# Normalised tiles of sequences one to three and seven k tiles turned by 32x32 blocks on VectorE, by way of DRAM, in a gated linear attention and MLP kernel

## The chip, the cores and the metric

The kernel runs on one core of one Trainium2 chip. A core has five engines with a queue each, and each takes its instructions in order: TensorE (PE in the profile: matrix products, and transposes as products with an identity; its weight loads are listed as PEld), VectorE (DVE), ScalarE (ACT), GpSimd (POOL) and SyncE (SP), which here issues every DMA. They wait for each other by semaphores. The metric is the device time of one execution in microseconds (us); the median of several executions is compared.

## The reference, cut to what matters

The input x has 4 sequences of 512 tokens with 512 features, in fp32. The layer is a chunked gated linear attention (4 heads of 128, chunks of 128 tokens), followed by a GEGLU MLP whose weights are 4-bit codes with scales. Both have a layer norm before them and a residual after.

```python
q = norm(x) @ Wq + bq;  k = norm(x) @ Wk + bk;  v = norm(x) @ Wv + bv     # 4 heads of 128
k = k / max(|k|, 1e-12)                        # per head
alpha = sigmoid(norm(x) @ Walpha + balpha);  beta = softplus(norm(x) @ Wbeta + bbeta)
# per chunk of 128 tokens, per head:
cla   = cumsum(log(alpha + 1e-6))
attn  = (qc @ kc.T) * beta.T * tril(exp(cla - cla.T))
y     = attn @ vc + (qc @ state.T) * exp(cla)
state = state * exp(cla_end) + vc.T @ (kc * beta * exp(cla_end - cla))
x1    = x + y
gate = norm(x1) @ Wg.T;  up = norm(x1) @ Wu.T            # 4096 wide
out  = x1 + (gelu_tanh(gate) * up) @ Wd.T
```

Two operands have to be turned for this, since TensorE contracts over partitions: a normalised tile (128 tokens on partitions by 512 features) is needed with the features on partitions, and so is a k tile (128 tokens by 4 heads of 128), for `qc @ kc.T`.

## The kernel before

The work is cut into 16 tiles of 128 tokens, (b, n) with b the sequence and n the chunk in it. The program is written in its final order by hand; nothing reorders it. The attention part runs steps p = 0 to 47: in sequence b, step 12b + j makes one product, `product_v(b, j)` for j = 0 to 3, `product_q(b, j - 4)` for j = 4 to 7, `product_k(b, j - 8)` for j = 8 to 11. After each product `behind(p)` places the rest of the work. The chunk with the running number c = 4b + n is worked off in steps 9 + 3c to 11 + 3c, by what p leaves when divided by three:

- p % 3 == 0: `chunk_lead` turns the chunk's k tile on TensorE (four transposes, L519, tile tpk) and ScalarE copies it to kT (L522); `chunk_decay` makes the decay matrix dm (ScalarE, GpSimd) and qc (GpSimd).
- p % 3 == 1: `turn` turns norm tiles on TensorE (L333: tp_f for the MLP's norm, tp_a for the first norm, four transposes each); ScalarE copies tp_a into hT (L348, two copies). `chunk_scores` (L586, tile sp) multiplies kT with q; VectorE multiplies the result with dm (L597). Loads of later tiles of x are issued here.
- p % 3 == 2: `chunk_sums` makes the state's update dp (L611) and the output yp (L640, L642); VectorE adds yp to the residual tile xr (L649), takes the second norm's statistics (L298 to L304), adds the state, and starts the first norm of a later tile (`first_norm`, L298 to L305). `settle` then normalises: hn_f and hn_a (L312). One slot of weight unpacking follows on VectorE (`unpack`, in the steps with p % 3 not 0, after p = 12), and then the next product's sums (L390 to L392 for v, L418 for k).

The first norm of a tile runs far ahead of its use: tile (1, n) in steps 2, 5, 8 and 8, tile (2, n) in steps 11, 14, 17 and 20, tile (3, n) in steps 23, 26, 29 and 32; their products begin in steps 12, 24 and 36.

SP's queue holds the DMAs in program order, and a DMA that waits holds all behind it. At most eight DMAs are under way: each one also waits for the eighth before it. SBUF tiles of 128x512 fp32 come from a list of 42 homes (`one_k`), taken from the front and given back at the end; PSUM has eight banks, taken in turn. From step 43 on the MLP is mixed in; it is a long run of products (L774, L818) with the weights unpacked beside them on VectorE.

Of the kernel before, what the change touches and what calls it, by code (L numbers as in the profile page):

```python
# [8 lines left out]
F32 = mybir.dt.float32  # L9
# [4 lines left out]
AF = mybir.ActivationFunctionType  # L14
ALU = mybir.AluOpType
# [6 lines left out]
P = 128  # L22
# [13 lines left out]
def f32(t):  # L36
    return t.bitcast(F32)
# [3 lines left out]
def tile_gated_linear_attention__then__nvfp4_geglu(  # L41
# [19 lines left out]
    nc = tc.nc  # L61
    B, T, D = x.shape
    H = D // P
    NCH = T // P
    NT = B * NCH
    KC = D // P
# [8 lines left out]
    dram = ctx.enter_context(tc.tile_pool(name="dram", bufs=1, space=DRAM))  # L75
# [199 lines left out]
    acc, hT, q_sb, k_sb, v_sb = {}, {}, {}, {}, {}  # L275
# [5 lines left out]
    def load(src, name):  # L281
        t = one_k.get(name)
        nc.sync.dma_start(f32(t), src)
        return t
# [7 lines left out]

    settled, turned = [], []

    def norm(src, key, use, parts=1, within=None):

        st = small.tile([P, 6], F32, tag="st", name=f"st_{key}")
        nc.vector.bn_stats(st, f32(src))  # L298
        if within:
            within()  # L300
        mv = small.tile([P, 2], F32, tag="mv", name=f"mv_{key}")
        nc.vector.bn_aggr(mv, st)
        rs = small.tile([P, 1], F32, tag="rs", name=f"rs_{key}")
        nc.vector.tensor_scalar(rs, mv[:, 1:2], 1e-5, None, ALU.add)  # L304
        nc.gpsimd.tensor_tensor(rs, rs, minus_half[:, :1], ALU.pow)  # L305

        def settle():

            hn = one_k.get(f"hn_{key}")
            w = D // parts  # L310
            for cols in (slice(i * w, (i + 1) * w) for i in range(parts)):
                nc.vector.tensor_scalar(  # L312
                    f32(hn)[:, cols].rearrange("p (c two j) -> p c two j", two=2, j=P),
                    f32(src)[:, cols].rearrange("p (c j two) -> p c two j", two=2, j=P),
                    mv[:, 0:1], rs, ALU.subtract, ALU.mult,
                )
            one_k.put(src)
            turned.append((hn, key, use))

        settled.append(settle)  # L320
# [6 lines left out]
    def turn(which, most=NT):  # L327
        for done in [t for t in turned if t[1][0] in which][:most]:
            turned.remove(done)
            hn, key, use = done  # L330
            tp = psum(f"tp_{key}")
            for k in range(KC):
                nc.tensor.transpose(tp[:, k * P : (k + 1) * P], f32(hn)[:, k * P : (k + 1) * P], ident)  # L333
            one_k.put(hn)
            use(tp)

    def first_norm(b, n, src, within=None):
        if n == 0:
            hT[b] = [two_k.get(f"hT{b}_{c}") for c in range(KC // 2)]

        soon = b == n == 0

        def use(tp):
            for c in range(KC // 2):
                to = f32(hT[b][c])[:, :, n * P : (n + 1) * P]
                new = tp[:, 2 * c * P : 2 * (c + 1) * P].rearrange("p (two t) -> p two t", two=2)
                for part in ((0, 1), (1, 2)) if soon else ((0, 2),):
                    nc.scalar.copy(to[:, slice(*part), :], new[:, slice(*part), :])  # L348

        norm(src, f"a{b}_{n}", use, 2 if soon else 1, within)  # L350

    def second_norm(b, n, src):
        def use(tp):
# [40 lines left out]
    def product_q(b, h):  # L394
# [10 lines left out]
            f32(q_sb[b][h // 2])[:, h % 2, :], pq, AF.Identity, bias=bq_sb[:, h : h + 1]  # L405
        )

    def product_k(b, n):

        pk = psum(f"pk_{b}_{n}")  # L410
        for k in range(KC):
            nc.tensor.matmul(  # L412
                pk, f32(hT[b][k // 2])[:, k % 2, n * P : (n + 1) * P], f32(wk[k // 2])[:, k % 2, :],
                start=(k == 0), stop=(k == KC - 1),
            )
        kt = one_k.get(f"k_{b}_{n}")
        k_sb[b, n] = kt
        nc.vector.tensor_tensor(f32(kt), pk, f32(bk_sb), ALU.add)  # L418
        return lambda: k_factors(b, n, kt)

    def k_factors(b, n, kt):
        sq = one_k.get(f"sq_{b}_{n}")
        sn = small.tile([P, H], F32, tag="ss", name=f"ss{b}_{n}")
        for h in range(H):
            hs = slice(h * P, (h + 1) * P)
            nc.scalar.activation(
                f32(sq)[:, hs], f32(kt)[:, hs], AF.Square, accum_out=sn[:, h : h + 1]
            )
# [74 lines left out]
    def gates_end(b):  # L503
        nc.vector.tensor_tensor(bdte[b], bdte[b], beta[b], ALU.mult)
# [8 lines left out]
    state, ch = {}, {}  # L513

    def chunk_lead(b, n):
        kT = one_k.get(f"kT_{b}_{n}")
        tp = psum(f"tpk_{b}_{n}")
        for h in range(H):
            nc.tensor.transpose(  # L519
                tp[:, h * P : (h + 1) * P], f32(k_sb[b, n])[:, h * P : (h + 1) * P], ident  # L520
            )
        nc.scalar.copy(f32(kT), tp)  # L522
        ch["kT"] = kT
# [38 lines left out]
    def chunk_values(b, n):  # L562

        brn, kwf = ss.pop((b, n))
        kt = k_sb[b, n]
        if n + 1 < NCH:
            kw = one_k.get(f"kw_{b}_{n}")
            nc.gpsimd.tensor_tensor(heads(f32(kw)), heads(f32(kt)), bc(kwf), ALU.mult)
# [129 lines left out]
    def behind(p):  # L698
        place[0] = p + 1
        b, j = divmod(p, 3 * NCH)  # L700
        chunk = chunk_of(p)
        first = b < B
        if not first:
            between_steps(p)
        left = chunk if p not in met else None
        if p % 3 == 0:
            if left:
                chunk_lead(*chunk)
            exps = gates_exp(b) if first and j == 3 else None
            if chunk and chunk[1] == 0:  # L710
                chunk_values(*chunk)
            if first and j == 6:
                exps = gates_sums(b)
            if left:
                chunk_decay(*chunk)
            if exps:
                exps()
        elif p % 3 == 1:
            turn("f")

            if p > 1:
# [12 lines left out]
        else:  # L734
            if first and j == 5:
                gates_ln(b)
            if chunk and not summed:
                sums, rest = chunk_sums(*chunk)
                sums()
                summed.append(rest)  # L740
            while summed:
                summed.pop()()
            for t in early.get(p, ()):
                first_norm(*t, xs.pop(t))
            if p + 1 < 3 * NCH * B:
                settle()
# [173 lines left out]
    with tc.manual_schedule():  # L920
# [3 lines left out]
        bv_sb, bk_sb = one_k.get("bv"), one_k.get("bk")  # L924
# [40 lines left out]
        blocks = mlp()  # L965
        p = 0
# [95 lines left out]
```

## Time and profile before

| what | value |
|---|---|
| median of 3 runs | 1308.09 us (1307.48 to 1310.34) |
| the profiled execution's own time | 1308.09 us |
| its span in the profile | 1306.1 us, 17024 instructions |
| TensorE busy | 1296.4 us, 99% |
| VectorE, ScalarE, GpSimd busy | 954.0 us (73%), 461.5 us (35%), 108.9 us (8%) |
| the three groups of transposes on TensorE (tp_a, tp_f, tpk) | 10.0, 9.7 and 9.6 us busy, 64 records each |
| ScalarE's copies of their results (hT, kT) | 10.3 us in 34, 9.3 us in 16 |
| DMA | 240.79 MB, mean 184 GB/s, 56.7% of 16 engines |

The profiled execution took the time of the median run, and its span leaves 2.0 us around it. A record's duration includes the time a product takes to run through the array, and that overlaps the next one: what a group of products takes from TensorE's row is the distance between starts, read in the order of time. Each fp32 transpose of 128x128 stands as two records in the groups, and as "x4" for four instructions in the order of time.

### The profile page before, as it was taken

Reading aid. Unit: us, or ns where it says so; the run is one execution under the profiler, and the core shown is the slowest. Engines: PE = TensorE matmul, PEld = TensorE weight load, DVE = VectorE, ACT = ScalarE, POOL = GpSimd, SP = SyncE. Lnnn points to the kernel's source line nnn. Section 1 sums busy time; section 2 is a strip of 40 time slices with the busy share of each in tenths; the row PEclk is TensorE's granted clock in tenths of the full one; section 3 lists DMA queues with packets and bytes.
Section 4 is the critical chain, followed back from the end, with each engine's and each line's share of the span. In section 5 each row is a group of like instructions: output and inputs, shape, how many; then the busy total and the mean of one; then the engine's idle time right before and its main releaser. Section 6 shows DMA issues by size and latency. Waiting matters only on the chain.

```text
span 1306.1 us, 17024 instructions
## 1 busy us (share of the span) xinstructions
PE 1296.4 (99%) x5808; PEld 1038.3 (79%) x5808; DVE 954.0 (73%) x1539; ACT 461.5 (35%) x908; POOL 108.9 (8%) x179
## 2 busy tenths in 40 slices
PE   9999999999999999999999999999999999999998
PEld 6677676778888888888888888888888888887886
DVE  3467665798777777777777777777777777777566
ACT  2443435753333333333333333333333333332332
POOL 1535263410000000000000000000000000000000
PEclk9999999999999999999999999999999999999999
DMA  5235446888555555555555555555555555555463
GB/s 194 82 108 173 123 128 211 266 272 261 184 184 187 187 185 183 187 186 184 185 186 186 186 187 184 186 184 187 183 186 186 188 183 186 185 177 197 169 248 128
DMA packets 176374, 240.79 MB, mean 184 GB/s; under 512 B 16096, under 2 KB 74784, under 8 KB 176288
## 3 DMA queue, kind: packets, MB, share of 16 engines
q1 hardware_dynamic: 176288, 239.72, 56.7%
q8 instruction: 45, 0.74, 0.2%
q14 instruction: 41, 0.34, 0.1%
HBM read 187.19 MB, written 52.46 MB: 183 GB/s over the span
## 4 chain that ended last, share of the span: by engine, by line
PE 96%; DMA 2%; DVE 2%; ACT 1%; issue 0%; SPq 0%; POOL 0%; DVEq 0%; ACTq 0%; POOLq 0%
PE pa L774 35%; PE p_d L818 26%; PE pb L774 17%; PE pq L400 4%; PE pk L412 4%; PE pva L375 2%; PE pvb L382 2%; PE sp L586 1%; PE yp L640 1%; PE dp L611 1%; DMA x<-h 1%; PE yp L642 1%; PE tp_a L333 1%; PE tp_f L333 0%; PE tpk L519 0%; DMA h<-g 0%
## 5 line engine op out<-in xcount | busy, mean ns | idle before, releaser
L774 PE MATMUL pa<-x,wgu 128*128 128x512 f32 x2048 | 507.1, 390 | 0.0
L774 PEld LDWEIGHTS pa<-x,wgu 128*128 128x128 f32 x2048 | 383.9, 188 | 79.0
L818 PE MATMUL p_d<-wd,i 128*128 128x512 f32 x1542 | 357.3, 390 | 2.3 <-DVE xr L649 0.6
L818 PEld LDWEIGHTS p_d<-wd,i 128*128 128x128 f32 x1542 | 288.4, 188 | 65.7 <-DVE i L798 2.1
L779 ACT ACTIVATE t<-pb 128x512 f32<-128x512 f32 x256 | 151.2, 591 | 358.9 <-PE pb L774 355.5
L774 PE MATMUL pb<-x,wgu 128*128 128x512 f32 x1024 | 275.3, 390 | 1.5 <-DMA x<-h 1.4
L780 DVE TENSOR_TENSOR t<-pa,t 128x512 f32<-128x512 f32 x256 | 176.5, 690 | 82.6 <-ACT t L779 76.9
L774 PEld LDWEIGHTS pb<-x,wgu 128*128 128x128 f32 x1024 | 192.3, 188 | 43.0 <-DMA x<-h 3.2
L826 DVE SCALAR_TENSOR_TENSOR acc<-p_d,acc 128x512 f32<-128x512 f32 (+1 forms) x137 | 93.4, 682 | 124.4 <-PE p_d L818 123.9
L794 ACT ACTIVATE i<-t 128x512 fp32r<-128x512 f32 x128 | 81.0, 633 | 194.2 <-DVE t L791 191.2
L786 ACT ACTIVATE t<-t 128x512 f32<-128x512 f32 x128 | 81.1, 634 | 135.8 <-DVE t L780 135.7
L798 DVE TENSOR_TENSOR i<-t,i 128x512 fp32r<-128x512 f32 x128 | 88.4, 690 | 25.9 <-ACT i L794 24.1
L830 DVE TENSOR_TENSOR acc<-acc,p_d 128x512 f32<-128x512 f32 x135 | 92.9, 688 | 14.1
L791 DVE SCALAR_TENSOR_TENSOR t<-t,t 128x512 f32<-128x512 f32 x128 | 88.6, 692 | 4.3
L799 DVE SCALAR_TENSOR_TENSOR i<-i,t 128x512 fp32r<-128x512 f32 x128 | 88.1, 689 | 0.0
L849 POOL TENSOR_TENSOR acc<-acc,last 128x512 f32<-128x512 f32 x1 | 1.3, 1295 | 1015.1 <-ACT last L848 1015.1
L400 PE MATMUL pq<-hT,wq 128*128 128x512 f32 x128 | 57.7, 595 | 0.0
L412 PE MATMUL pk<-wk,hT 128*128 128x512 f32 x128 | 57.4, 593 | 0.0
L400 PEld LDWEIGHTS pq<-hT,wq 128*128 128x128 f32 x128 | 23.3, 191 | 23.5 <-issue 23.4
L412 PEld LDWEIGHTS pk<-wk,hT 128*128 128x128 f32 x128 | 23.2, 191 | 23.4 <-issue 23.4
L183 DVE TENSOR_TENSOR wgu<-wgu,wgu 128x1024 fp32r<-128x1024 f32 x32 | 39.0, 1218 | 0.0
L171 DVE SCALAR_TENSOR_TENSOR w_gu<-i_gu,sc_gu 128x1024 f32<-128x1024 f16 x32 | 38.9, 1216 | 0.0
(117 smaller groups left out, 913.7 us busy)
## 6 DMA issues: line engine op xcount, KB each, us to landing
x<-h SPq DMA_DIRECT2D x420, 256.0 KB
acc<-acc SPq DMA_DIRECT2D x256, 256.0 KB
h<-g SPq DMA_DIRECT2D x48, 256.0 KB
x<-in_x SPq DMA_DIRECT2D x16, 256.0 KB
pk_gu<-in_gate_p SPq DMA_DIRECT2D x32, 128.0 KB
sc_gu<-in_gate_s SPq DMA_DIRECT2D x64, 64.0 KB
pk_gu<-in_up_p SPq DMA_DIRECT2D x32, 128.0 KB
sc_gu<-in_up_s SPq DMA_DIRECT2D x64, 64.0 KB
```

Source lines behind the costliest of these rows:

```text
L400: nc.tensor.matmul(pq, f32(wq[k // 2])[:, k % 2, h * P : (h + 1) * P], f32(hT[b][k // 2])[:, k % 2, :], start=(k == 0), stop=(k == KC - 1),)
L412: nc.tensor.matmul(pk, f32(hT[b][k // 2])[:, k % 2, n * P : (n + 1) * P], f32(wk[k // 2])[:, k % 2, :], start=(k == 0), stop=(k == KC - 1),)
L774: nc.tensor.matmul(o, w3[j][:, k % 2, c * P : (c + 1) * P], x[j * KC + k], start=(j == js[0] and k == 0), stop=(j == js[-1] and k == KC - 1),)
L779: nc.scalar.activation(f32(t), pb, AF.Copy, scale=-1.0 / ONE_E)
L780: nc.vector.tensor_tensor(f32(t), pa, f32(t), ALU.add)
L786: nc.scalar.activation(f32(g), f32(g), AF.Gelu_apprx_tanh, scale=ONE_E)
L791: nc.vector.scalar_tensor_tensor(f32(u), f32(g), ONE_E, f32(u), ALU.mult, ALU.mult)
L798: nc.vector.tensor_tensor(il, f32(u), f32(ih), ALU.subtract)
L799: nc.vector.scalar_tensor_tensor(im, f32(ih), ONE_E, f32(u), ALU.mult, ALU.subtract)
L818: nc.tensor.matmul(banks[key_][:, part], inter[i][j][:, n * P : (n + 1) * P], wd[ms[i] // 2][j][:, ms[i] % 2, part], start=(i == 0 and j i ...
L826: nc.vector.scalar_tensor_tensor(a, banks[n, False, part.start][:, part], ONE_E, a, ALU.mult, ALU.add)
L830: nc.vector.tensor_tensor(a, a, banks[n, True, 0], ALU.subtract)
```

## The change

Twelve first-norm tiles, those of sequences 1 to 3, and seven k tiles, those with n > 0 among the first ten chunks, are no longer turned on TensorE. In their place:

- the tile is written with its 32-column blocks sorted for the trip (`crossed`): hn by two VectorE instructions of 128x256 in place of one of 128x512, k by the same one addition with a blocked access pattern;
- `cross` stores it to a DRAM tile (one DMA, 256 KB, in pieces of 512 B);
- `land` loads it back so that each 32-partition group receives its blocks (four DMAs of 64 KB). For a norm tile they are issued in the step after the store; for a k tile in step p % 3 == 1, two products ahead of `chunk_lead`;
- `turn_blocks` turns the 32x32 blocks on VectorE: two instructions of 128x256 into hT, two products behind the loads, or one of 128x512 into kT, in `chunk_lead`.

The ScalarE copies into hT and kT of these tiles go, and so do their PSUM banks. The k sums, the squares for the k norm and GpSimd's kw product get a blocked access pattern for all 16 chunks.

```diff
+    def crossed(t):
+        return t.rearrange("p (w k i) -> p k w i", w=KC, i=32)
+
+    def cross(src, key, use):
+        way = dram.tile([KC, P, P], F32, tag=f"way_{key}", name=f"way_{key}")
+        nc.sync.dma_start(way.rearrange("w p m -> p w m"), f32(src).rearrange("p (w m) -> p w m", m=P))
+        return way, key, use
+
+    def land(way, key, use):
+        t = one_k.get(f"way_{key}")
+        for a in range(KC):
+            nc.sync.dma_start(f32(t)[:, a * P : (a + 1) * P], way[:, a * 32 : (a + 1) * 32, :])
+        return lambda: use(t)
+
+    def turn_blocks(t, *to):
+        new = f32(t).rearrange("p (a k i) -> p k a i", a=KC, i=32)
+        done = 0
+        for part in to:
+            n = part.shape[1]
+            nc.vector.transpose(part.rearrange("p k (a j) -> p k a j", j=32), new[:, done : done + n])
+            done += n
+        one_k.put(t)
...
@@ norm, in settle
+            if way:
+                for c in range(2):
+                    nc.vector.tensor_scalar(
+                        crossed(f32(hn)).rearrange("p (c two) w i -> p c two w i", c=2)[:, c],
+                        f32(src).rearrange("p (c w i two) -> p c two w i", c=2, w=KC, two=2)[:, c],
+                        mv[:, 0:1], rs, ALU.subtract, ALU.mult,
+                    )
+                one_k.put(src)
+                coming.append(cross(hn, key, way))
+                one_k.put(hn)
+                return
...
@@ first_norm
+        def way(t):
+            turn_blocks(t, *(f32(hT[b][c])[:, :, n * P : (n + 1) * P] for c in range(KC // 2)))
-        norm(src, f"a{b}_{n}", use, 2 if soon else 1, within)
+        norm(src, f"a{b}_{n}", use, 2 if soon else 1, within, way if b > 0 else None)
...
+    def far(b, n):
+        return 0 < n and NCH * b + n < 2 * NCH + 2
...
@@ product_k
-        nc.vector.tensor_tensor(f32(kt), pk, f32(bk_sb), ALU.add)
+        nc.vector.tensor_tensor(heads_of(kt, far(b, n)), in_blocks(pk), in_blocks(f32(bk_sb)), ALU.add)
+        if far(b, n):
+            ways[b, n] = cross(kt, f"k{b}_{n}", lambda t: turn_blocks(t, heads(f32(ch["kT"]))))
...
@@ chunk_lead
+        if far(b, n):
+            ch["kT"] = one_k.get(f"kT_{b}_{n}")
+            ways.pop((b, n))()
+            return
...
@@ behind, p % 3 == 0
+            come.extend(land(*t) for t in coming)
+            coming.clear()
@@ behind, p % 3 == 1
+            after = chunk_of(p + 2)
+            if after and far(*after):
+                ways[after] = land(*ways[after])
@@ behind, p % 3 == 2, after the chunk's sums, ahead of first_norm
+            while come:
+                come.pop(0)()
```

More of the change, by code (lines that the diff above doesn't have):

```diff
@@ L293, in tile_gated_linear_attention__then__nvfp4_geglu, with norm @@
     settled, turned = [], []
-    def norm(src, key, use, parts=1, within=None):
+    coming, come = [], []
+    def crossed(t):
[17 more added lines that the diff above has]
+        one_k.put(t)
+    def norm(src, key, use, parts=1, within=None, way=None):
         st = small.tile([P, 6], F32, tag="st", name=f"st_{key}")
@@ L406, in product_q, with in_blocks, heads_of @@
         )
+    def far(b, n):
+        return 0 < n and NCH * b + n < 2 * NCH + 2
+    ways = {}
+    def in_blocks(a):
+        return a.rearrange("p (h w i) -> p h w i", h=H, i=32)
+    def heads_of(t, blocks):
+        return crossed(f32(t)) if blocks else in_blocks(f32(t))
     def product_k(b, n):
@@ L426, in k_factors @@
             nc.scalar.activation(
-                f32(sq)[:, hs], f32(kt)[:, hs], AF.Square, accum_out=sn[:, h : h + 1]
+                f32(sq)[:, hs].rearrange("p (w i) -> p w i", i=32), heads_of(kt, far(b, n))[:, h],
+                AF.Square, accum_out=sn[:, h : h + 1],
             )
@@ L567, in chunk_values @@
             kw = one_k.get(f"kw_{b}_{n}")
-            nc.gpsimd.tensor_tensor(heads(f32(kw)), heads(f32(kt)), bc(kwf), ALU.mult)
+            nc.gpsimd.tensor_tensor(
+                in_blocks(f32(kw)), heads_of(kt, far(b, n)),
+                kwf.unsqueeze(2).unsqueeze(3).to_broadcast([P, H, KC, 32]), ALU.mult,
+            )
             ch["kw"] = kw
```

## The prediction

> **What bounds the kernel now.** I read the page's busy times first, then the shares of the chain that ended last, and then both engines in order of time around one turned chunk.
>
> ```profile
> PE 1296.4 (99%) x5808; PEld 1038.3 (79%) x5808; DVE 954.0 (73%) x1539; ACT 461.5 (35%) x908; POOL 108.9 (8%) x179
> PE 96%; DMA 2%; DVE 2%; ACT 1%; issue 0%; SPq 0%; POOL 0%; DVEq 0%; ACTq 0%; POOLq 0%
> ```
>
> TensorE has work 99% of the span and is 96% of the chain. Every instruction taken from its row is time, unless a later one now waits for its operand. So two questions remain: what does a turned tile cost on TensorE's row, and who delivers the operand late? TensorE around chunk 5, tile (1, 1), in order of time:
>
> ```profile
> 120.07 0.60 PE L519 MATMUL tpk<-ident,k 128*128 128x128 f32 x4
> 120.50 1.95 PE L375 MATMUL pva<-wva,hT 128*128 128x264 f32 x8
> 122.29 1.89 PE L382 MATMUL pvb<-wvb,hT 128*128 128x256 f32 x8
> 124.01 0.60 PE L333 MATMUL tp_f<-ident,hn_f 128*128 128x128 f32 x4
> 124.45 0.60 PE L333 MATMUL tp_a<-ident,hn_a 128*128 128x128 f32 x4
> ```
>
> Starts count, not durations: tpk moves the row on by 120.50 - 120.07 = 0.43 us, tp_a by 0.44 us (124.45 to sp at 124.89). VectorE over the same steps:
>
> ```profile
> 116.76 0.69 DVE L649 TENSOR_TENSOR xr<-xr,yp 128x512 f32<-128x512 f32 x1 [1.09 <-PE yp L640]
> 118.50 0.68 DVE L617 COPY state<-dp 128x512 f32<-128x512 f32 x1
> 119.10 0.68 DVE L298 BATCH_NORM_STATS2 st_a<-x 128x6 f32<-128x512 f32 x1
> 120.12 0.55 DVE L312 TENSOR_SCALAR hn_f<-xr,mv_f,rs_f 128x512 f32<-128x512 f32 x1
> 121.11 0.55 DVE L312 TENSOR_SCALAR hn_a<-x,mv_a,rs_a 128x512 f32<-128x512 f32 x1 [0.45 <-POOL rs_a L305]
> 121.57 1.22 DVE L171 SCALAR_TENSOR_TENSOR w_d<-i_d,sc_d 128x1024 f32<-128x1024 f16 x1
> 122.71 0.42 DVE L390 TENSOR_TENSOR v<-pva,bv 128x264 f32<-128x264 f32 x1
> 123.38 0.15 DVE L392 TENSOR_TENSOR zs<-pvb,bab_sb 128x8 f32<-128x8 f32 x1
> 124.22 0.42 DVE L391 TENSOR_TENSOR v<-pvb,bv 128x248 f32<-128x248 f32 x1 [0.35 <-PE pvb L382]
> ```
>
> The engine with 73% busy time has a closed run here: from the end of yp at 116.7 to 124.2 it waits for TensorE not once, and ends 0.7 us before sp starts. ScalarE delivers kT in the old form, outside this run. The new kT turn stands inside it, behind the v sums, with sp next on TensorE.
>
> **What leaves.** 12 + 7 = 19 tiles by 0.436 us (mean of 0.43 and 0.44) are 8.3 us of TensorE's row. TensorE is busy for all of 20 to 185 us, where the 19 stand, so all of it is path. ScalarE loses 24 hT copies (0.64 us a pair) and seven kT copies (0.58 us), 11.7 us; it was 69 us busy in those 165, so that is worth nothing. PSUM has fewer claimants; TensorE's waits named no bank, so nothing again.
>
> **What VectorE gets.** No row shows a block transpose. The nearest rows are whole passes over the same shape: for 128x512, the k sum L418 at 689 ns and the norm L312 at 546 ns; a following instruction starts about 0.09 us before the end, so they advance the queue by 0.60 and 0.46 us. For 128x256 they are the v sums, 0.34 us from start to start. I take 0.60 and two times 0.34, since a transpose writes every element once and the slower row is the safer one. The bounds are 0.46 from below, and from above twice the slowest 128x512 row, 1.38. Splitting hn in two costs 0.19 us: the one such pair in the trace (tile (0, 0)) took 0.74 us against 0.55. The total is 12 x (0.68 + 0.19) + 7 x 0.60 = 14.6 us, where VectorE was 98.4 of 165 us busy. Room enough, but what counts is the closed run.
>
> **Where the wait forms.** In a far chunk VectorE now has, between yp and kT, 0.68 (hT turn, ahead of st_a) and 0.19 (hn_a), then the kT turn, 0.69 to its end, and some 0.06 for the semaphore: 1.62 us. TensorE meanwhile gets to sp 0.87 us sooner, without tpk and tp_a. I read off where VectorE had finished what now stands before kT, and sp's start less 0.87:
>
> For (0, 1): 62.07 and 64.67 - 0.87 = 63.80, a room of 1.73; two tiles are turned in the step before, so 2.30 is added: wait 0.57. For (0, 2): 78.08 and 79.13, room 1.05: wait 0.57. For (0, 3): 93.19 and 95.28, room 2.09: none. For (1, 1): 123.45 and 124.02, room 0.57: wait 1.05. For (1, 2): 138.85 and 139.35, room 0.50: wait 1.12. For (1, 3): 153.34 and 155.51, room 2.17: none. For (2, 1), without a new first norm and tp_a: 181.35 and 184.24, room 2.89: none. The pattern has a cause: n = 3 stands in steps with a q product and little unpacking in front, while (1, 1) and (1, 2) have a 1.22 us unpacking instruction there. Sum of the waits: 3.3 us. Behind the waiting sp stand the next product, dp and yp on TensorE; the dm product on VectorE follows sp, has the whole next product as cover (over 3.4 us), and hands nothing on.
>
> **SP and the transfers.** Rows that price them:
>
> ```profile
> 133.74 1.28 SPq L201 DMA_DIRECT2D sc_gu<-in_gate_s  x2
> 125.33 1.70 SPq L360 DMA_DIRECT2D h<-g  x3
> 66.00:66.50 0.50, 0.50 (x4) 0.43 (x3) 0.50 (x2) 0.00 (x0) 0.50 (x1) 1.00 0.97 280
> ```
>
> A store of the same form (h<-g) issues in about 0.5 us and a 64 KB load of 512 B pieces in up to 0.64; I take 0.5. A turned tile is then 2.5 us of SP, 19 of them 48 us in 160, between issues that were mostly waits. At the 280 GB/s of the last line 256 KB take 0.9 us; 38 trips add 34 us to a mean DMA share of 0.39 in those 165 us, so 0.60. One trip: the h stores' data ran from 66.0, 0.9 us after issue at 65.05, so 2.2 us to a landed store, 2 us for four issues, 1.6 us for the last load: 6 us. A norm tile has two products (about 10 us) from its store to its turn, a k tile two from its loads, so later than the ramp they land first. The store for a tile waits for VectorE (hn, k) and holds the h stores, x and weight loads behind it by up to 4 us; their users come 12 us later or more. ScalarE's squares and GpSimd's qc wait for a few of these DMAs when they inherit a home; over 17 homes are free throughout, so it has landed.
>
> The ramp is tighter. The store of (1, 1) waits for hn_a at 36.4 us and now precedes six weight loads (3.6 us, from 100.63 to 104.20 for the same six), so its own loads end at 42.5 and land at 44.5. VectorE wants them after k (0, 0), at 42.0, and stands 2.5 us. That delays the norms of (1, 2) and (1, 3), GpSimd's pow, kw and vb and then dm to 52.4, and the dm product to 53.1; yp comes at 53.9. So 0.8 us are left: nothing by this working, up to 4 us if the loads come some 3 us later or the chain repeats at the loads of (1, 3), which land 56.8 for a turn at 57. GpSimd's blocked kw (1.04 us before) and the blocked squares I leave at their rows; a quarter more on kw eats 0.3 of the 0.8.
>
> **Sum.** Against the profiled execution, 1308.09 us (equal to the median): -8.3 + 3.3 + 0 = -5.0, so 1303.1 us. The MLP and the handover to it (waits for x at 260 to 275 us) follow step 36 unchanged and move as a block.
>
> **A rule against the change.** In the rows a transpose on TensorE moves its queue 0.109 us (0.436 / 4). The Trainium skill, "VectorE: DVE Perf Modes", section "The three transpose paths", gives 390 ns on TensorE and 311 ns on VectorE for 128x128 in bf16, and "Rules for kernel authors" sends a 128x128 transpose to TensorE when PSUM will do. Taken at the page's 311 ns four times, an estimate of 1.24 us for a k tile and for a norm tile, the formula below gives waits of 10.6 us and a kernel 2.3 us slower; no run here shows yet whether a 512-wide transpose pays that start four times.
>
> **Rivals.** (a) All is covered: the waits vanish because VectorE turns blocks faster than 0.46, or its run has give that I don't see. Then 1308.1 - 8.3 = 1299.8. At 0.46 the waits are still 2.0 us, 1301.8. For it speaks that room is under 1 us short everywhere; against it that VectorE's run is closed. (b) The ramp: loads in SP's queue late, 1 to 4 us more, 1304 to 1307. For it: six DMAs ahead and a 2.5 us stand; against it: 0.8 us spare. (c) Slower: the block transpose is slower than a pass. With X for the advance of a 128x512 turn (two halves X + 0.08), the waits sum to 13 X - 5.5 once X is over 0.84, where (0, 3) and (1, 3) wait too. From X = 1.06 on the gain is gone; at 1.38 the waits are 12.5 with (2, 1) joining, and the kernel takes 1312.3. For it: nothing in the trace moves data across partitions on VectorE; against it: its passes all run near one element per ns and lane (689 ns for 512, 1.22 us for 1024).
>
> **Numbers.** The likeliest, with its waits between 2 and 4.5 us: 0.45, range 1301.5 to 1304.5. (a) 0.17. (b) 0.21, half of it above 1305.5. (c) 0.13, 0.08 of it slower by over 0.2%. Something else, 0.04. A measurement tells about 0.2%, 2.6 us, from no change: faster 0.45 + 0.17 + 0.10 = 0.72, same 0.11 + 0.05 + 0.01 = 0.17, slower 0.08 + 0.03 = 0.11. The range takes (a) whole and leaves out most of (c): 1299.6 to 1308.6.
>
> **What would show it.** TensorE's row: 76 transposes fewer, sp's weight load waiting for kT on VectorE in (0, 1), (0, 2), (1, 1), (1, 2), 0.5 to 1.2 us each, in none with n = 3. Block transposes at 0.69 us (128x512) and 0.42 us (128x256). A VectorE stand for DMA at about 42 us. It is wrong if the transposes take over 1 us, if yp waits for dm near 54 us, or if TensorE idles after 185 us more than before.

## The result, and the profile after

The changed kernel takes 1322.3 us (median of 4 runs, 1321.67 to 1323.53), the kernel before 1308.08 us: ratio 1.0107, 95% interval 1.0089 to 1.0124. It is slower by 14.2 us, where the prediction was 5 us faster and a range up to 1308.6. The profiled execution of after has a span of 1319.9 us, 13.8 us more than the 1306.1 us of before, so it shows the difference well.

The page of the changed kernel, busy times, the granted clock in 40 slices, and the chain that ended last:

```profile
PE 1296.2 (98%) x5732; PEld 1035.1 (78%) x5732; DVE 972.9 (74%) x1582; ACT 451.5 (34%) x877; POOL 111.0 (8%) x179
...
PEclk9989899999999999999999999999999999999999
...
PE 86%; DMA 5%; DVE 3%; SPq 2%; ACT 1%; issue 1%; POOL 0%; DVEq 0%; POOLq 0%; ACTq 0%
```

TensorE has 76 instructions fewer and yet the same busy time (at a lower clock the rest takes longer); two slices of its clock are at eight tenths; and DMA, VectorE and SP's queue together are a tenth of the chain, where TensorE alone had 96%. The loss is in the first 200 us, in three stretches. TensorE there, by stretches (after the bounds: length, TensorE busy and its instructions, granted clock, DMA share, GB/s):

```profile
20.00:200.00 180.00, 165.89 (x682) 0.95 0.55 161
...
50.00:55.00 5.00, 3.61 (x13) 1.00 0.93 297
55.00:60.00 5.00, 3.84 (x17) 0.66 0.44 132
...
65.00:70.00 5.00, 1.96 (x11) 1.00 0.70 203
70.00:75.00 5.00, 3.66 (x13) 0.51 0.42 141
75.00:80.00 5.00, 5.00 (x27) 0.81 0.36 110
```

Between 20 and 200 us TensorE idles 180 - 165.89 = 14.1 us; before, it did not idle there at all. Behind an idle stretch the clock falls to half: 0.66 over 5 us is 3.4 us at 0.5, 0.51 and 0.81 are 6.8 us. The whole trace has four such phases, 17.1 us at half clock, in which 8.5 us of work is lost. The account closes: -8.3 us (19 tiles off the row) + 14.1 + 8.5 = +14.3 us, against 13.8 measured in the span.

What TensorE waited for, in order of time:

```profile
54.31 1.16 PE L677 MATMUL dp<-v,kw 128*128 128x128 f32 x8 [1.39 <-POOL kw L631]
56.63 2.07 PE L706 MATMUL yp<-vb,dm 128*128 128x128 f32 x8 [1.16 <-DVE dm L663]
68.00 0.63 PE L374 MATMUL tp_f<-ident,hn_f 128*128 128x128 f32 x4 [1.67 <-DVE hn_f L353]
71.34 2.04 PE L652 MATMUL sp<-q,kT 128*128 128x128 f32 x8 [2.71 <-DVE kT L320]
90.37 1.16 PE L652 MATMUL sp<-q,kT 128*128 128x128 f32 x8 [1.62 <-DVE kT L320]
133.24 0.63 PE L374 MATMUL tp_f<-ident,hn_f 128*128 128x128 f32 x4 [0.34 <-DVE hn_f L353]
136.91 1.13 PE L652 MATMUL sp<-q,kT 128*128 128x128 f32 x8 [3.04 <-DVE kT L320]
155.48 2.07 PE L652 MATMUL sp<-q,kT 128*128 128x128 f32 x8 [2.19 <-DVE kT L320]
```

The four waits of sp stand in (0,1), (0,2), (1,1) and (1,2), where the prediction had them, but they are 9.6 us, not 3.3. The other 4.6 us stand at places that had been given nothing. VectorE shows why:

```profile
47.87 0.77 DVE L320 STREAM_TRANSPOSE hT<-way_a 128x256 f32<-128x256 f32 x2 [5.86 <-DMA way_a<-way_a]
62.24 0.77 DVE L320 STREAM_TRANSPOSE hT<-way_a 128x256 f32<-128x256 f32 x2 [1.09 <-DMA way_a<-way_a]
65.65 0.77 DVE L320 STREAM_TRANSPOSE hT<-way_a 128x256 f32<-128x256 f32 x2 [2.63 <-DMA way_a<-way_a]
86.38 1.45 DVE L343 TENSOR_SCALAR hn_a<-x,mv_a,rs_a 128x256 f32<-128x256 f32 x2 [0.44 <-POOL rs_a L335]
130.88 0.77 DVE L320 STREAM_TRANSPOSE hT<-way_a 128x256 f32<-128x256 f32 x2 [2.54 <-DMA way_a<-way_a]
136.06 0.70 DVE L320 STREAM_TRANSPOSE kT<-way_k 128x512 f32<-128x512 f32 x1
```

The transposes cost what was predicted (0.70 us, and 0.77 us for a pair of halves). But VectorE stands for the loads of norm tiles four times, 12.1 us in all, and for k loads once (0.70 us, ahead of the kT turn at 70.48 us); hn_a takes twice its time here and at 150.95 us. One tile's loads alone on the DMA engines, by the microsecond:

```profile
27.00:28.00 1.00, 1.00 (x4) 0.43 (x3) 0.00 (x0) 0.32 (x1) 0.00 (x0) 1.00 0.28 83
29.00:30.00 1.00, 1.00 (x4) 0.52 (x3) 0.00 (x0) 0.00 (x0) 0.00 (x0) 1.00 0.24 71
```

The last two columns are the DMA share and GB/s: a quarter of the engines' time, 71 to 83 GB/s, for over 3 us. The prediction had put these 256 KB at 280 GB/s.

### The profile page after: what moved, and what is told of

It reads as the page before. It is cut to its first block, busy times and chain, and to the rows that moved or that the text cites. A ratio compares the mean times of both kernels' runs of the same rounds, so it can differ in the third digit from the quotient of the medians.

```text
span 1319.9 us, 17034 instructions
## 1 busy us (share of the span) xinstructions
PE 1296.2 (98%) x5732; PEld 1035.1 (78%) x5732; DVE 972.9 (74%) x1582; ACT 451.5 (34%) x877; POOL 111.0 (8%) x179
## 4 chain that ended last, share of the span: by engine, by line
PE 86%; DMA 5%; DVE 3%; SPq 2%; ACT 1%; issue 1%; POOL 0%; DVEq 0%; POOLq 0%; ACTq 0%
PE pa L847 34%; PE p_d L891 25%; PE pb L847 17%; PE pq L444 3%; PE pk L468 2%; DMA x<-h 2%; PE pva L419 1%; SPq L311 1%; PE pvb L426 1%; PE sp L652 1%; DMA way_a<-way_a 1%; DMA way_k<-way_k 1%; DMA way_a<-hn_a 1%; DMA xr<-in_x 1%; PE yp L706 1%
## 5 line engine op out<-in xcount | busy, mean ns | idle before, releaser
L180 DVE SCALAR_TENSOR_TENSOR wgu<-wgu,w_gu 128x1024 fp32r<-128x1024 f32 x32 | 38.9, 1216 | 0.0
```

## The experiments

The theory: TensorE's idle time has three sources (A: the kT turn stands at the end of VectorE's closed run; B: norm tiles land late, since their loads use a quarter of the DMA engines; C: VectorE's run meets GpSimd's passes, and these slow it), and the half clock follows from the waits. Rivals: the number of DMAs and SP's order as such; VectorE's load alone; a clock that falls for another reason. All kernels compute the whole reference.

### One kind of tile at a time

k_tiles_only:

```
-        norm(src, f"a{b}_{n}", use, 2 if soon else 1, within, way if b > 0 else None)
+        norm(src, f"a{b}_{n}", use, 2 if soon else 1, within)
```

> Only the seven k tiles are turned through DRAM and VectorE; all norm tiles are turned on TensorE as in the kernel before. My theory (TensorE's idle time comes from the closed run on VectorE and from norm tiles that land late, and each idle stretch of about 3 us is followed by a phase at half clock): 7 tiles by 0.436 us leave TensorE's row, -3.05 us. The k loads are issued a whole product before their turn, so VectorE stands for none of them for more than 1 us. Without the hT turn and the split of hn the rooms for the kT turn are 2.17, 1.49, 1.01 and 0.94 us in (0,1), (0,2), (1,1), (1,2), against the 0.75 us that it needs: no wait of sp over 0.3 us, no phase at half clock between 20 and 185 us, 1305 us (1304 to 1307). Rival one (a block transpose on VectorE ahead of sp, or the DRAM trips on SP's queue, cost time as such): sp waits in the same chunks, about 7/19 of the loss of 22.5 us against the covered kernel, +8 - 3 = 1313 us. Rival two (the clock falls for another reason than the waits): 1305 us plus about 8 us of half clock.

Measured: 1306.23 us, ratio 0.9981 (0.9969 to 0.9994); span 1303.4. In the first 200 us, only the sp of (1,2) waits, for 0.55 us, and the clock stays at 1.00. 7 x 0.436 = 3.05 us less and 0.55 back are -2.5; the span says -2.7. The gain per tile is as priced, and a block transpose behind landed data costs TensorE next to nothing.

norm_tiles_only:

```
     def far(b, n):
-        return 0 < n and NCH * b + n < 2 * NCH + 2
+        return False
```

> Only the twelve norm tiles are turned through DRAM and VectorE; the k tiles are turned on TensorE and copied by ScalarE as in the kernel before. My theory (the norm tiles land late, and VectorE stands for them): 12 tiles by 0.436 us leave the row, -5.2 us; the stands at 42 us (about 5.9 us) and at 61 us stay, TensorE idles some 2.5 us at 50 to 60 us and 2 to 4 us at 65 to 75 us, a half-clock phase of 3.4 us (1.7 us lost) follows each; at 128 us the stand of 2.5 us is taken up by what the kT turn leaves free. Together 1303 + 2.5 + 3 + 3.4 = 1312 us (1308 to 1315). Rival (the kT turn inside VectorE's run is the whole cause, and the late loads are covered): 1303 us, without idle stretches of TensorE over 1 us.

Measured: 1308.35 us, ratio 0.9996 (0.9984 to 1.0009). TensorE's waits in the first 200 us, in order of time:

```profile
55.93 1.60 PE L677 MATMUL dp<-v,kw 128*128 128x128 f32 x8 [2.46 <-POOL kw L631]
58.25 2.08 PE L706 MATMUL yp<-vb,dm 128*128 128x128 f32 x8 [0.72 <-DVE dm L663]
```

Behind them the granted clock is 0.65 from 55 to 60 us and 0.67 from 60 to 65, 6.8 us at half. So the late norm tiles cost 3.2 us of waiting and 3.4 us of half clock at the ramp, more than the 5.2 us that the twelve tiles give. The stands at 63 and 66 us are there too (0.6 and 2.7 us), but no kT turn stands behind them, and TensorE doesn't notice: that part of my expectation was too dear by 3 us. The two halves alone are -2.0 and +0.2 us, together they are +14.2: they cost through each other. The next runs ask what does it, VectorE's run or the loads.

### The same loads by all engines

wide_loads:

```
-        for a in range(KC):
-            nc.sync.dma_start(f32(t)[:, a * P : (a + 1) * P], way[:, a * 32 : (a + 1) * 32, :])
+        for w in range(KC):
+            nc.sync.dma_start(
+                f32(t)[w * 32 : (w + 1) * 32, :].rearrange("j (a m) -> j a m", a=KC),
+                way[w].rearrange("(a j) m -> j a m", a=KC),
+            )
```

> The changed kernel; only the four loads of a tile are cut in another way: one for each block of 32 partitions of the target instead of one for each block of 32 tokens, so that the outermost loop of the source runs over 32 rows instead of 4 blocks. The same bytes, the same 512-byte pieces, the same number of issues on the same queue in the same order. My theory (the loads are late because they run on a quarter of the DMA engines: share 0.25 to 0.28 and 81 to 84 GB/s in the trace, against 260 to 294 GB/s of the stores beside them): 256 KB take about 1 us instead of 3.2, the DMA share beside the loads goes to 0.8 or more, the stands of VectorE at 61 and 128 us vanish and that at 42 us falls to 2 to 3.5 us. TensorE's waits shrink from 14 us to the 4 to 6 us of the kT turn in VectorE's closed run, with at most one or two half-clock phases: 1306.5 us (1304 to 1311). Rival one (the loads are late by their place in SP's queue and by four issues per tile): stands and time as they are, 1320 to 1324 us. Rival two (loads are a small part, VectorE's run is the bound): 1316 to 1320 us.

Measured: 1308.87 us, ratio 1.0002 (0.9988 to 1.0016). Same bytes, pieces, issues and order, and 13.4 us of the 14.2 are gone. The first tile's loads, as above (DMA share and GB/s last):

```profile
27.00:28.00 1.00, 1.00 (x3) 0.39 (x3) 0.00 (x0) 0.69 (x1) 0.00 (x0) 1.00 0.51 143
```

The same four turns on VectorE, in order of time (that of 130.88 us is now at 119.58):

```profile
45.84 0.77 DVE L323 STREAM_TRANSPOSE hT<-way_a 128x256 f32<-128x256 f32 x2 [3.44 <-DMA way_a<-way_a]
59.06 0.77 DVE L323 STREAM_TRANSPOSE hT<-way_a 128x256 f32<-128x256 f32 x2 [0.84 <-DMA way_a<-way_a]
60.30 0.77 DVE L323 STREAM_TRANSPOSE hT<-way_a 128x256 f32<-128x256 f32 x2 [0.47 <-DMA way_a<-way_a]
119.58 0.76 DVE L323 STREAM_TRANSPOSE hT<-way_a 128x256 f32<-128x256 f32 x2
```

The share is 0.51, where it had been 0.24 to 0.28, and 0.51 is more than four engines of 16 can give. It does not reach the 0.8 that I expected: four issues now take 1.75 us in SP's queue (64 KB each, 0.44 us), and that pace is 150 GB/s. The stand that had been at 128 us is gone, the two at 61 to 65 us are 0.84 and 0.47 us, that at 42 us is 3.44 us. What is left on TensorE is the kT turn:

```profile
54.60 1.16 PE L709 MATMUL yp<-vb,dm 128*128 128x128 f32 x8 [0.40 <-DVE dm L666]
65.36 1.13 PE L655 MATMUL sp<-q,kT 128*128 128x128 f32 x8 [2.09 <-DVE kT L323]
81.69 1.16 PE L655 MATMUL sp<-q,kT 128*128 128x128 f32 x8 [1.63 <-DVE kT L323]
125.59 1.13 PE L655 MATMUL sp<-q,kT 128*128 128x128 f32 x8 [0.94 <-DVE kT L323]
142.45 1.36 PE L655 MATMUL sp<-q,kT 128*128 128x128 f32 x8 [2.16 <-DVE kT L323]
```

7.2 us, and one half-clock phase behind the last (1.7 us): -8.3 + 7.2 + 1.7 = +0.6; the median says +0.7. B is shown. It does not cost this much alone: norm_tiles_only has the same narrow loads and loses 0.2 us, so it takes the kT turn behind the late tiles as well. The rival that blamed SP's order and the number of issues falls.

### kT turned earlier, with the loads as they were

kt_early (the load and the turn leave their old places, in p % 3 == 1 and in `chunk_lead`):

```
@@ def behind, p % 3 == 0, behind the norm tile's loads @@
+            after = chunk_of(p + 3)
+            if after and far(*after):
+                ways[after] = land(*ways[after])
@@ def behind, p % 3 == 2, ahead of everything @@
+            after = chunk_of(p + 1)
+            if after and far(*after):
+                ch["kT"] = one_k.get("kT_%d_%d" % after)
+                ways.pop(after)()
```

> The changed kernel with narrow loads as they are, but the k tile of a chunk is loaded one product earlier and turned one product earlier, at the point where VectorE stands about 1.1 us for yp; so sp no longer stands behind a kT turn at the end of VectorE's run. My theory (two causes that add: kT at the end of the run, and norm tiles that land late): the waits of sp for kT go (0,1: 2.7, 0,2: 1.6, 1,1: 3.0, 1,2: 2.2 us), what is left is the idle 2.5 us at 50 to 60 us, the wait of tp_f for hn_f behind the late norm tile in (0,1), 1.5 to 3 us, and two or three phases of half clock: 1309 us (1306 to 1314). Rival (the late norm tiles are the whole cause, kT only shows them): the waits move to tp_f with nearly the same length, 1317 us or more.

Measured: 1347.94 us, ratio 1.0293 (1.0269 to 1.0318): both expectations failed. VectorE at the first turn:

```profile
69.04 0.71 DVE L320 STREAM_TRANSPOSE kT<-way_k 128x512 f32<-128x512 f32 x1 [11.23 <-DMA way_k<-way_k]
```

SP's queue ahead of it (start, length, number of issues):

```profile
56.56 4.91 SPq L311 DMA_DIRECT2D way_a<-way_a  x8
61.52 3.30 SPq L311 DMA_DIRECT2D way_k<-way_k  x4
```

The k loads stand behind eight loads of norm tiles on the same few engines, 768 KB in all, and are issued at 61.5 us for a turn wanted at 58. VectorE stands for k loads at all seven turns, 49.7 us in sum. So the experiment says nothing for or against A; it shows that an earlier place in the order is worth nothing while the data land where they did, and that the earlier place must be read against the loads' times, which I had not done.

### kT turned earlier, with wide loads

wide_mid is wide_loads, the turn leaves `chunk_lead`, and:

```
@@ def behind, p % 3 == 2 @@
             while come:
                 come.pop(0)()
+            after = chunk_of(p + 1)
+            if after and far(*after):
+                ch["kT"] = one_k.get("kT_%d_%d" % after)
+                ways.pop(after)()
@@ def far @@
-        return 0 < n and NCH * b + n < 2 * NCH + 2
+        return 0 < n and 1 < NCH * b + n < 2 * NCH + 2
```

> Wide loads as before; the kT turn is moved from behind the v sums to just behind the hT turn, ahead of the norm, in VectorE's order, and chunk (0,1), whose loads are not landed by then in the trace of wide_loads, is turned on TensorE again. 18 tiles leave the row: -7.85 us. My theory (the waits of sp that are left in wide_loads, 2.1, 1.6, 0.9 and 2.2 us, come from where kT stands in VectorE's run, nothing else): sp waits for kT nowhere; hn_f, which had 3.3 us of room before, still comes ahead of tp_f; in (0,1) at most 0.5 us is left of the stands for the norm tiles at 59 to 60 us; no half-clock phase. 1300.2 + 0.5 + 0.4 = 1301 us (1299.5 to 1304). Rival one (VectorE's run as a whole is too long, so the wait goes to the next user, tp_f or the bank of the v sums): waits of the same length on other instructions, 1306 us or more. Rival two (the k loads come too late for the earlier place): stands of VectorE for the k loads of over 1 us in (1,1) and (1,2), 1305 us or more.

Measured: 1303.95 us, ratio 0.9967 (0.9956 to 0.9978), no phase at half clock. TensorE's waits:

```profile
83.71 0.49 PE L707 MATMUL yp<-vb,dm 128*128 128x128 f32 x2 [1.27 <-DVE dm L664]
98.92 0.49 PE L707 MATMUL yp<-vb,dm 128*128 128x128 f32 x2 [0.56 <-DVE dm L664]
143.73 0.49 PE L707 MATMUL yp<-vb,dm 128*128 128x128 f32 x2 [1.18 <-DVE dm L664]
```

sp waits nowhere, so its waits did come from where kT stood. But rival one is half right: 3 us come back one user later, at yp, since VectorE's run as a whole is as long as it was, and with yp at the ramp (0.27 us) and tp_f at 122.25 us (0.40 us) the waits are 3.7 us: -7.85 + 3.7 = -4.2, the span says -4.3. VectorE also stood 1.24 and 1.99 us for k loads.

wide_mid_soon issues the loads of the k tiles of n = 2 and 3 one product earlier:

```
@@ def behind, p % 3 == 0, behind the norm tile's loads @@
+            after = chunk_of(p + 3)
+            if after and far(*after) and after[1] > 1:
+                ways[after] = land(*ways[after])
@@ def behind, p % 3 == 1 @@
-            if after and far(*after):
+            if after and far(*after) and after[1] == 1:
```

> wide_mid, with the loads of the k tiles of n = 2 and 3 issued one product earlier (with the norm tile's loads), so that VectorE finds them landed. My theory (what is left in wide_mid, yp waiting 1.27 us for the dm product in (0,2), comes from VectorE's stand of 1.24 us for the k loads at 73 us; the 1.18 us in (1,2), where there was no such stand, from GpSimd beside VectorE): no stand for k loads but the one of 2 us in (1,1); yp's wait in (0,2) falls to 0.3 us or less, that in (1,2) stays over 0.8 us: 1304 - 1.1 = 1302.9 us (1301.5 to 1304). Rival (more loads ahead of the norm's turn delay that turn instead): VectorE stands for the norm tiles, 1304 us or more.

Measured: 1302.07 us, ratio 0.9948 (0.9936 to 0.9961): faster than the kernel before. A gain over wide_mid is not shown: the intervals overlap, and the spans of the two profiled executions are both 1301.8 us. yp's wait in (0,2) went from 1.27 to 0.33 us with the stand, that in (1,2) stayed at 1.19, as expected.

wide_mid_scalar is wide_mid_soon and gives GpSimd's decay of the state and its vb to ScalarE:

```
-                nc.gpsimd.tensor_tensor(
-                    heads(f32(new)), heads(f32(state[b])), bc(td[b][:, n * H : (n + 1) * H]), ALU.mult
-                )
+                for h in range(H):
+                    hs = slice(h * P, (h + 1) * P)
+                    nc.scalar.activation(
+                        f32(new)[:, hs], f32(state[b])[:, hs], AF.Copy,
+                        scale=td[b][:, n * H + h : n * H + h + 1],
+                    )
...
-        if b < B - 1:
-            nc.gpsimd.tensor_tensor(heads(f32(vb)), heads(f32(v_sb[b, n])), bc(brn), ALU.mult)
-        else:
-            for h in range(H):
+        for h in range(H):
```

> wide_mid_soon, and the decay of the state and vb are done by ScalarE in four parts each (the form that the last sequence has for vb) instead of GpSimd, which keeps the select of dm, qc and kw. My theory (a pass on GpSimd beside a pass on VectorE slows both): the unpacking instructions behind hn_a in (0,2) and (1,2) go from 1.21 and 1.74 us to 0.68 and 1.21 us, hn_a stays at 1.45 us since qc is still beside it, yp's wait in (1,2) falls from 1.18 us to 0.4 to 0.8 us: 0.5 us less than wide_mid_soon, 1302.4 us (1301 to 1303.5). Rival (ScalarE, with eight instructions more in a chunk, becomes late with the exponents of dm or with g): yp or tp_f wait for longer, 1304 us or more.

Measured: 1302.92 us, ratio 0.9953 (0.9940 to 0.9967), not to be told from wide_mid_soon. yp's wait in (1,2) is 0.46 us, but the two unpacking instructions still take 1.22 and 1.74 us, beside the qc that is left on GpSimd. The expected time came, and the expected mechanism at another place: the pair of unpacking instructions one step earlier, which in wide_mid_soon ran beside GpSimd's kw and vb,

```profile
127.19 2.47 DVE L162 TENSOR_SCALAR i_gu<-pk_gu 128x512 int32<-128x512 int32 x2
```

takes 0.75 us here, and VectorE comes to xr 0.98 us earlier (129.34 instead of 130.32 us).

### GpSimd beside VectorE

wide_calm is wide_loads with the decay on ScalarE, as just shown, and qc on VectorE behind the dm product:

```
-                nc.gpsimd.tensor_tensor(
-                    heads(f32(qc))[:, 2 * c : 2 * c + 2, :], f32(q_sb[b][c])[:, :, toks],
@@ def chunk_scores, behind the dm product @@
+                nc.vector.tensor_tensor(
+                    heads(f32(ch["qc"]))[:, 2 * c : 2 * c + 2, :], f32(q_sb[b][c])[:, :, toks],
```

> Wide loads as before; GpSimd's two products qc are done on VectorE behind the dm product, and the decay of the state by ScalarE in four parts, so that GpSimd has only the select of dm left beside VectorE's run. My theory (in (0,2) and (1,2) VectorE's pair hn_a takes 1.45 us instead of 0.73, and the unpacking behind it 1.21 and 1.75 us instead of 0.69 and 1.22, because GpSimd runs qc and the decay at that time): these instructions go back to 0.73 to 0.85, 0.69 and 1.22 us, sp's waits in (0,2) and (1,2) fall from 1.63 and 2.16 us to 0.5 to 0.8 and 1.0 to 1.3 us, the half-clock phase behind (1,2) goes: 1308.9 - 2.1 - 1.7 = 1305 us (1304 to 1306.5). Rival (the durations come from something else, such as DMA traffic or operands): durations and waits as they are, 1308 to 1311 us.

Measured: 1309.39 us, ratio 1.0002 (0.9990 to 1.0014). The unpacking instructions went to 0.68 and 1.21 us, as expected, but hn_a to 1.76 us instead of 0.8: with qc gone, vb moved up beside it. So vb had to go as well. wide_calmer is wide_calm with vb on ScalarE, as in wide_mid_scalar.

> As wide_calm, and vb too is done by ScalarE in four parts, since in wide_calm it moved into the place beside hn_a that qc had left (hn_a then took 1.76 us): GpSimd keeps only the select of dm (0.64 us) beside VectorE's run. My theory (a pass of GpSimd beside a pass of VectorE slows it): hn_a in (0,2) and (1,2) takes 0.73 to 1.1 us, i_gu and wd behind it 0.68 and 1.21 us, sp waits 0.6 to 1.0 and 1.1 to 1.5 us there instead of 1.63 and 2.16 us, no half-clock phase behind (1,2): 1308.9 - 1.9 - 1.7 = 1305.3 us (1304 to 1307). Rival one (hn_a's 1.45 us has another cause than GpSimd): it stays there, 1308 us or more. Rival two (ScalarE, now with three passes more, becomes late itself): other waits, 1308 us or more.

Measured: 1307.98 us, ratio 0.9991 (0.9981 to 1.0000). VectorE in (0,2) and (1,2), in order of time:

```profile
79.27 1.04 DVE L346 TENSOR_SCALAR hn_a<-x,mv_a,rs_a 128x256 f32<-128x256 f32 x2 [0.44 <-POOL rs_a L338]
80.23 0.68 DVE L167 TENSOR_SCALAR i_gu<-i_gu 128x1024 int32<-128x1024 int32 x1
...
138.55 1.03 DVE L346 TENSOR_SCALAR hn_a<-x,mv_a,rs_a 128x256 f32<-128x256 f32 x2 [0.44 <-POOL rs_a L338]
139.51 1.21 DVE L180 SCALAR_TENSOR_TENSOR wd<-wd,w_d 128x1024 fp32r<-128x1024 f32 x1
```

TensorE's waits there:

```profile
82.32 1.16 PE L650 MATMUL sp<-q,kT 128*128 128x128 f32 x8 [0.68 <-DVE za L517]
...
142.13 1.16 PE L650 MATMUL sp<-q,kT 128*128 128x128 f32 x8 [1.21 <-DVE za L517]
```

hn_a, i_gu and wd fall by 0.4, 0.5 and 0.5 us, and the waits of sp from 1.63 and 2.16 to 0.68 and 1.21 us (za is the instruction right behind kT, named in its place). C is shown for these two chunks. The time fell less than expected: the gain of 1.9 us and the phase behind (1,2) came, but here the clock fell once more at the handover, where TensorE waits in all kernels (here 1.02 and 0.59 us in a row, in wide_loads 0.42 and 0.59): the mean clock from 200 to 300 us is 0.98, about 1.7 us. -8.3 + 5.6 + 1.7 = -1.0, measured -1.1.

### The clock by itself

held_1, held_2 and held_4 are the kernel before, with one, two or four copies that only keep sp waiting:

```
         kT = ch.pop("kT")
+        for _ in range(2 if n in (1, 2) and b < 2 else 0):
+            nc.scalar.copy(f32(kT), f32(kT))
```

> The kernel before, with one copy of kT onto itself on ScalarE ahead of sp in chunks (0,1), (0,2), (1,1), (1,2), behind ScalarE's hT copies; nothing else changes. TensorE then waits for sp about 0.96 + 0.1 + 0.5 = 1.5 us in each of the four chunks, 6 us in all. My theory of the clock (a wait of 1.6 us left it alone in the changed kernel, stretches of 3 us halved it for 3.4 us or 6.8 us): no half-clock phase, 1308.1 + 6 = 1314 us. Rival (each wait over 1.2 us halves the clock for 3.41 us and costs 1.7 us more): 1321 us.

> As held_1 with two copies in each of the four chunks: waits of sp of 1.3 to 1.55 us as in held_1 plus about 0.6 us for one copy more, so 1.9 to 2.2 us each, 8 us in all. It asks at what length the clock falls. In wide_loads a wait of 2.09 us left it at 1.00 and one of 2.16 us was followed by 3.41 us at half. If the length of one wait decides, with its bound at about 2.1 us: one or two phases, 1308.5 + 8.3 + 1.7 to 3.4 = 1319 us (1317 to 1321). If it is decided by how a wait falls into windows of a fixed beat: any number from none to four, with phases behind some waits and not behind longer ones; 1316.5 to 1323.5 us.

> The same with four copies in each of the four chunks: waits of sp of about 0.96 + 0.1 + 2.0 = 3 us each, 12 us in all. My theory of the clock: each of the four waits is followed by at least one phase of 3.41 us at half clock, 1.7 us lost, 6.8 us in all or more: 1308.1 + 12.2 + 6.8 = 1327 us (1325 to 1332), with four phases in the trace that have no DMA of a turned tile near them. Rival (the half clock of the changed kernel came from something else, the DMA trips or VectorE's transposes): clock 1.00 throughout, 1320 us.

| kernel | four waits, us | half-clock phases in the first 200 us | time, us | ratio (95%) |
|---|---|---|---|---|
| held_1 | 1.30 to 1.55, sum 5.7 | none | 1315.11 | 1.0053 (1.0034 to 1.0073) |
| held_2 | 1.95 to 2.20, sum 8.3 | 4 | 1321.87 | 1.0096 (1.0071 to 1.0121) |
| held_4 | 3.25 to 3.50, sum 13.4 | 4 | 1329.35 | 1.0159 (1.0134 to 1.0183) |

One wait of held_2 on TensorE:

```profile
66.23 1.86 PE L588 MATMUL sp<-q,kT 128*128 128x128 f32 x8 [1.95 <-ACT kT L586]
```

The stretch that holds it, and the next (length, TensorE busy, granted clock, DMA share, GB/s):

```profile
63.09:66.50 3.41, 1.46 (x12) 1.00 0.32 89
66.50:69.92 3.42, 3.42 (x13) 0.50 0.98 292
```

There are no DRAM trips or block transposes in these kernels, and the clock falls all the same: the half clock follows from the waits, and the rival falls. For held_4, 13.4 + 4 x 1.7 = 20.2 us, measured +20.9. held_2's four times lie at 1318.6 and 1319.1, 1324.7 and 1324.8 us: two groups, nearly 6 us apart, for the same program. The profiled run, with four phases, is of the dearer group (8.3 + 6.8 = 15.1 us, and 1324.7 is 15.6 above before). The cheaper two have fewer phases: the granted clock on record is 0.999 and 0.997 for them, 0.995 for each of the dearer two.

What decides is how a wait falls into a fixed beat. In every trace the times between two changes of the granted clock are whole multiples of 3.41 us (in the changed kernel 51.20, 3.41, 10.24, 6.83, 61.44, 3.41 and 13.65 us: 15, 1, 3, 2, 18, 1 and 4 beats). Two waits of wide_loads show it, that of 2.09 us, cut by the end of a beat into 1.47 and 0.62 us, and that of 2.16 us, which lies in one:

```profile
61.34:64.75 3.41, 1.94 (x11) 1.00 0.99 281
64.75:68.16 3.41, 2.79 (x17) 1.00 0.76 249
...
139.84:143.25 3.41, 1.25 (x12) 1.00 0.52 137
143.25:146.66 3.41, 3.41 (x8) 0.50 0.54 138
```

Over all 14 traces here, every full-clock beat in which TensorE idled 1.9 us or more (18 of them) was followed by half clock, none with 1.55 us or less was, and of ten between 1.58 and 1.87 us five were; what parts these is not shown. Waits in one beat add up: 1.39 and 1.16 us in the changed kernel (2.25 us of them in one beat), 1.02 and 0.59 us in wide_calmer.

## Why the prediction was wrong

**What leaves, -8.3 us: right.** k_tiles_only and wide_mid, where the waits are few, agree with 0.436 us a tile to 0.2 us in the span.

**What VectorE gets: right.** 0.60 us of advance and twice 0.34 were assumed for the turns; 0.704 us for one 128x512 and 0.77 us for a pair were measured, against the 0.69 and 0.76 that go with them. So rival (c) falls. The weighed rule (four starts of a 128x128 transpose) does not hold for this shape: it would be 1.24 us.

**Where the wait forms, +3.3 us: the places right, the sizes short.** All four chunks were named, and the three with none. With every turned tile landing sooner (wide_loads) the four waits sum to 6.8 us. Two of them lose 0.95 us each when GpSimd is kept away (wide_calmer): 0.68 and 1.21 us, where 0.57 and 1.12 were predicted; with (1,1) at 0.94 against 1.05 the arithmetic of the closed run was good to 0.1 us. (One reading in it was off and entered no sum: VectorE does wait for TensorE ahead of 124.22 us, 0.35 us for pvb, as the row shown there says.) What it lacked was that hn_a and the unpacking behind it now run beside GpSimd's select, qc and decay. Before, in (1,2), the select started 1.5 us behind hn_a (136.51 us), since ScalarE made dm's exponents behind its kT copy (136.17 us; the exponents from 136.65). Without that copy they begin at 148.87 us, two microseconds ahead of hn_a (150.95 us), and the select starts with it:

```profile
138.00 0.69 POOL L538 TENSOR_SCALAR_AFFINE_SELECT dm<-dm 128x512 f32<-128x512 f32 x1 [1.53 <-ACT dm L534]
...
150.88 0.64 POOL L601 TENSOR_SCALAR_AFFINE_SELECT dm<-dm 128x512 f32<-128x512 f32 x1
```

The hT turn ahead of hn_a is not needed for this: in k_tiles_only, which has none, the two start at 134.35 and 134.42 us, and wd takes 1.74 us. So the relief of ScalarE, put at nothing, moved GpSimd's passes onto VectorE's run. And (0,1) waits 2.1 instead of 0.57 us, 1.3 us of it VectorE's stands for norm tiles in the same run.

**SP and the transfers, 0 us: the step that failed.** "At the 280 GB/s of the last line 256 KB take 0.9 us" and "1.6 us for the last load" were read off transfers of another form (stores and x loads). The loads of a turned tile ran at 71 to 83 GB/s alone. So "later than the ramp they land first" was false at 64 and at 128 us (stands of 2.6 and 2.5 us), and the stand at 42 us was 5.9, not 2.5. With the loads cut so that more engines serve them, 13.4 us of the loss of 14.2 go. The share of about 0.25 is what 4 of 16 engines would give, and the form fits: the source's outermost loop has four blocks, in wide_loads 32 rows. The Trainium skill, "DMA: Bandwidth & Descriptors", section "Rules for kernel authors", says that an outermost dimension of fewer than 16 confines a DMA to at most that many engines; the trace agrees nearly (0.24 to 0.28), and the prediction had passed over it. Rival (b) had the mechanism, late loads, but kept it to the ramp and at 1 to 4 us.

**The clock: no step at all.** 8.5 us. The waits of before, at most 0.8 us between 20 and 300 us, had left the clock at 1.00, and I took a wait's price to be its length. The Trainium skill, "TensorE: Matmul & The Clock Gate", Part 1, puts half clock behind an idle window of about 3.4 us; the phases of 3.41 us agree, but here 1.95 us of waiting in one such stretch were enough.

Of the error of 19.2 us (1322.3 - 1303.1), 8.5 are the clock and 14.1 - 3.3 = 10.8 the waits, up to 0.1 us of rounding.

## What to carry to other kernels

Price a DMA by a row of the same access form, and look at the outermost dimension of both its sides before taking a bandwidth from another row: here four loads of 64 KB ran at a quarter of the engines' time, and swapping two loops was worth 13 us. When an engine off the path gets work inside a closed run, walk that run with every stand and every neighbour that may slow it, and put the turn whose user is next at the front of the run, after its data and not before. On TensorE, 1.9 us of idle time in one beat of 3.41 us, in one wait or in two, cost 1.7 us more here, so a few waits of 2 to 3 us cost much more than the same time in small ones far apart.

## What was not expected of the hardware

- Granted clock: the length of a wait alone does not decide. Waits of 3.25 us and over always lowered it in held_4; around 2 us, 1.95 and 2.01 us did (held_2), 2.09 (wide_loads) and 2.14 us (wide_calmer) did not, since the end of a beat cut them (1.47 and 0.62, 0.75 and 1.45 us in a beat).
- A VectorE pass beside a GpSimd pass is lengthened, mostly by about half a microsecond: i_gu 0.68 to 1.21 us, wd 1.21 to 1.74, the hn_a pair 0.73 to 1.45 or 1.76, the pair of i_gu beside kw and vb 0.75 to 2.47; GpSimd's decay took 2.02 instead of 1.04 us. The Trainium skill, "SBUF — State Buffer", section "Who interferes with whom", has the two share, in some of VectorE's forms, a port pair that one holds for a whole instruction while the other is blocked. The lengths fit a block rather than a sharing: in wide_mid_scalar, where only qc was left, wd starts at 136.28 us within qc, which ends at 136.95, and ends 1.07 us behind that, nearly its whole length of 1.21 us. So the mean load (GpSimd is busy 8% of the span) says little; what counts is whether a pass of the other runs at the start.
- Cut as in wide_loads, four loads of 64 KB go at the pace of their issues on SP, 0.44 us each: 143 GB/s in the best microsecond of the first tile, where 64 KB in 0.44 us are 150.
